# Gates and values of seven sequences by seven block products in a recurrent-attention block

## The chip, the cores and the metric

The kernel runs on one core of one Trainium2 chip. The metric is the device time of one execution in microseconds (us). A core has TensorE (PE, matrix products; its weight loads are listed apart as PEld), VectorE (DVE), ScalarE (ACT), GpSimd (POOL) and SyncE (SP, which here issues most DMAs). Each engine takes its instructions in the order in which they were traced and waits on semaphores for the others.

## The reference

Eight sequences of 1024 positions and 512 channels are normalized to `xn`. An attention without softmax over positions, with three decay rates and a gate, gives `s`; a feed-forward block whose weights are looked up in a table of 16 entries gives `g`; the result is `x + s * g`. The part that the change touches:

```python
q = x @ Wq                                  # x is the normalized input, 512 -> 128
gate = softmax(x @ Wg, axis=-1)             # 512 -> 3
for i in range(3):
    k = x @ Wk[i]; v = x @ Wv[i]            # 512 -> 128 each
    w = decay[i] ** max(t - s - 1, 0) * (later > earlier)
    scores = einsum('btd,bsd->bts', q, k) * w
    blended += gate[..., i:i+1] * einsum('bts,bsd->btd', scores, v)
s = blended @ Wo * out_scale
```

All arithmetic is in float32.

## The kernel before

Phase 1 (`phase_1`, L719) makes q^T, k^T, values and gates, runs the attention in chunks of 128 positions, from the last chunk to the first, and looks up the feed-forward weights. Phase 2 (L813) is the feed-forward block, with products of blocks nested twice, and the final sum.

Phase 1 has nine rounds, the passes of the loop over b at L759. In round b, `newer` projects sequence b, `older` runs the chunks of sequence b-1, `ending` finishes the projection of sequence b-1, `following` begins sequence b+1, and `build_some` adds steps of the table look-ups, which run on VectorE. A round has eight passes k (chunk c = 7 - k), and each pass three slots. All of these are generators, advanced by one step at fixed places of a slot, so the order of every engine's work is written out by hand and then held (`keep_order`). `defer(n, f)` issues f at the n-th later `tick`, of which there is one at each slot.

What the change and the steps of the prediction touch:

- `transpose` (L449) turns a chunk of the normalized input into `xnT` by four transposes (tile pt).
- `values` (L455): four matmuls of a chunk give 387 columns, three times 128 values and three gate logits (tile pv, L459), and ScalarE copies them into `v_sb` (L462). `newer` calls it in the third slot of every pass.
- `softmax` (L464), once for each half of 512 positions, makes the gates from the last three columns. VectorE and ScalarE do it in two steps, in the second and third slot of a half's first pass. Then `write` (L481) stores them transposed in DRAM by a DMA of single words on SP. Only for one half of sequence 0 does TensorE transpose them (`turn`, L485). A DMA on SP (L498) later spreads them over the partitions (tile ga).
- `features` (L500) makes q^T and k^T of a half by seven block products instead of eight (Strassen's scheme in Winograd's form). The matrix of weights is cut into 2 by 2 blocks, `xnT` likewise; t1 to t4 are sums of blocks of `xnT` (VectorE), s1 to s4 of weights (GpSimd). Each product is four matmuls of 256 columns (L520), into one of four PSUM banks pa, pb, pe, pc; copies on ScalarE and three-operand sums on VectorE (L552, L555) carry them on. `features(1)` runs in passes 4 to 7 of its own round, `features(0)` as `ending` in passes 0 to 3 of the next. A half's t1 is in the second slot of its first pass, product 5, which reads t1, in the third.
- `chunks` (L639), one step in each slot. First: pk, three transposes of k, copied to ks with a scale on ScalarE (L673). Second: psc = k^T q for three decays (L677), which VectorE weights into pr (L679); then `gated(c - 1)` multiplies gates and q for the next chunk (ga, L652, on VectorE; qb, L656, on GpSimd). Third: pu (L687), the update of the state; po (L701), first from the state, then from pr and the values; its copy into bl (L702) and, every four chunks, a DMA of bl on ScalarE's queue (L704).

In a slot the order is: `newer`, `following`, `older`, look-ups in the first; `ending` (two steps), `newer`, look-ups, `older`, look-ups in the second; `ending`, `newer`, `older` in the third.

Of the kernel before, what the change touches and what calls it, by code (L numbers as in the profile page):

```python
# [9 lines left out]
F32 = mybir.dt.float32  # L10
# [7 lines left out]
P = 128  # L18
# [30 lines left out]
def recurrent_block(ctx: ExitStack, tc, x, wq, wk, wv, wo, wg, decay_logits, out_scale, lut, gidx, uidx, didx, out):  # L49
# [33 lines left out]
    NQ = NO // 4  # L83
    EPS = 1e-5
# [24 lines left out]
    def more_weights(wvg_sb, wqk_sb):  # L109
        nc.scalar.dma_start(out=wvg_sb[:, :, NI * D :], in_=wg.rearrange("(c p) d -> p c d", p=P))  # L110
        for i in range(NI):
            nc.scalar.dma_start(
                out=wvg_sb[:, :, i * D : (i + 1) * D], in_=wv[i].rearrange("(c p) d -> p c d", p=P)
            )
# [46 lines left out]
    zero = const.tile([NI, P], F32)  # L161
# [7 lines left out]
    def tables(room):  # L169
# [8 lines left out]
        nc.gpsimd.memset(e_c, float(P))  # L178
        nc.gpsimd.memset(zero, 0.0)
# [222 lines left out]
    def project(b, pools, sides, kept):  # L402
# [5 lines left out]
        xp, xnp, tp, att = pools  # L408
        wvg_sb, wqk_sb, wqs = sides
        xnT = xnp.tile([P, NV, T], F32, name=f"xnT{b}", tag="xnT")  # L410
        mean, rstd, shift = (small.tile([P, NC], F32, name=f"{k}{b}", tag=k) for k in ("mean", "rstd", "shift"))
        v_sb = att.tile([P, NC, NI * D + NI], F32, name=f"v{b}", tag="v")
        gt = v_sb[:, :, NI * D :]
# [9 lines left out]
        def statistics(c):  # L423
# [10 lines left out]
            else:  # L434
                junk = small.tile([P, V], BF16, name=f"junk{b}_{c}", tag="junk", bufs=1)
# [19 lines left out]
        def values(c):  # L455

            pv = p_c.tile([P, NI * D + NI], F32, name=f"pv{b}_{c}", tag="c")
            for v in range(NV):
                nc.tensor.matmul(  # L459
                    pv, lhsT=xnT[:, v, ts(c, P)], rhs=wvg_sb[:, v, :], start=(v == 0), stop=(v == NV - 1)  # L460
                )
            nc.scalar.copy(v_sb[:, c, :], pv)  # L462

        def softmax(hf):  # L464
# [15 lines left out]

            def write():  # L481
# [3 lines left out]
            def turn():  # L485
# [3 lines left out]
                gs = small.tile([n * NI, P], F32, name=f"gs{b}_{hf}", tag="gs", bufs=1)  # L489
# [3 lines left out]
            ga = gates[-1]  # L493
            if (b, hf) == (0, 1):
# [3 lines left out]
            defer(6, lambda: nc.sync.dma_start(out=ga, in_=there.partition_broadcast(P)))  # L498

        def features(hf):  # L500
# [14 lines left out]
            pa, pb, pe, pc = (p_a.tile([P, 2, H], F32, name=f"{r}{b}_{hf}", tag=r) for r in ("pa", "pb", "pe", "pc"))  # L515
# [12 lines left out]

            there = xs_d[b][:, :, ts(hf, H)]
            nc.vector.tensor_tensor(t1, b12, b11, ALU.subtract)  # L530
            yield
            product(pa, 1, True)
            nc.scalar.copy(pb, pa)
            nc.vector.tensor_tensor(t2, b22, t1, ALU.subtract)
            nc.sync.dma_start(out=there[:, 0:4, :], in_=xnT[:, :, ts(2 * hf, H)])
            yield
            product(pe, 5, True)
            nc.scalar.copy(c21, pe)
            nc.vector.tensor_tensor(t3, b22, b12, ALU.subtract)
            nc.sync.dma_start(out=there[:, 4:8, :], in_=xnT[:, :, ts(2 * hf + 1, H)])  # L540
            yield
            product(pb, 6)
            nc.scalar.copy(pc, pb)
            nc.scalar.copy(c12, pb)
            nc.vector.tensor_tensor(t4, b21, t2, ALU.subtract)
            defer(2, lambda: nc.sync.dma_start(out=there[:, 8:16, :], in_=ts_.rearrange("p a b u -> p (a b) u")))
            yield
            product(pa, 2)
            nc.scalar.copy(c11, pa)
            yield  # L550
            product(pc, 7)
            nc.vector.tensor_tensor(c22, pc, c21, ALU.add)  # L552
            yield
            product(pe, 3)
            nc.vector.tensor_tensor(c12, pe, c12, ALU.add)  # L555
            yield
            product(pc, 4)
            nc.scalar.copy(c21, pc)
            yield
# [25 lines left out]
        yield  # L585
        before = 2 if b == 0 else 3
        lag = 1 if b == 0 else 0
        for k in range(NC):
# [8 lines left out]
            if b == 0 and k == 0:  # L597
                warm_up(5)
            yield
            if k == NC // 2:  # L600
# [943 lines left out]
```

## Time and profile before

| | us |
|---|---|
| median of the three runs (2082.22 to 2082.50) | 2082.42 |
| profiled execution | 2085.11 |
| its span, first to last instruction | 2083.3 |
| phase 1 in it, to the first product of phase 2 | 586.9 |
| rounds 1 to 7, from the first psc of sequence 0 (47.25) to that of sequence 7 (552.83) | 505.6 |
| round 8, from there to the end of phase 1 | 34.1 |

A row of a group reads: line, engine, operation, output <- inputs, shapes, count | busy us, mean ns of one | idle us of the engine just before them, and what ended it. Matmuls overlap, so the mean of one is longer than the distance between two starts. A row of the cut by time gives, for each engine, its busy us in that stretch and the number of its instructions, then TensorE's granted clock, the share of the DMA engines and GB/s. A row of the timeline gives the start, the length and the number of merged instructions. A row of the waits gives who waited for whom, us in total, times and the longest.

### The profile page before, as it was taken

What the parts mean: (1) busy time and instruction counts of PE and PEld (TensorE: products, weight loads), DVE (VectorE), ACT (ScalarE), POOL (GpSimd) and SP (SyncE); (2) the same over time, 40 slices, a digit from 0 to 9 for tenths busy, and PEclk for the clock granted to TensorE, in tenths of its full rate; (3) what the DMA queues carried; (4) which work ended last, traced back from release to release, by engine and by line L of the source; (5) the groups of instructions that cost most, each with busy time, mean ns of one, the idle gap of its engine ahead of it and who ended that gap; (6) DMA issues with size and microseconds to landing.
All of it is one profiled execution on the core that took longest, in us unless ns stands there. A gap on an engine that the chain in (4) does not pass through costs nothing.

```text
span 2083.3 us, 32914 instructions
## 1 busy us (share of the span) xinstructions
PE 2068.4 (99%) x12043; PEld 1755.3 (84%) x12043; DVE 1462.5 (70%) x2246; ACT 944.1 (45%) x2133; POOL 1043.8 (50%) x1042
## 2 busy tenths in 40 slices
PE   9999999999999999999999999999999999999999
PEld 7887888788888888897888888888978888797887
DVE  8989898788458775675577557656755765675567
ACT  4767766676444424423442442344144324423531
POOL 4554665244356446516543751755275255627442
PEclk9999999999999999999999999999999999999999
DMA  9866778756764734463464447345544734464442
GB/s 231 157 176 181 188 192 178 202 126 185 168 225 154 249 142 155 168 243 133 155 228 160 154 154 261 129 160 192 198 153 153 261 129 151 170 232 144 150 162 104
DMA packets 178494, 367.23 MB, mean 176 GB/s; under 512 B 37871, under 2 KB 113278, under 8 KB 178334
## 3 DMA queue, kind: packets, MB, share of 16 engines
q1 hardware_dynamic: 161734, 338.11, 53.0%
q10 hardware_dynamic: 12120, 12.34, 1.9%
q0 software_dynamic: 4480, 14.68, 1.7%
q8 instruction: 96, 1.57, 0.3%
q14 instruction: 64, 0.52, 0.1%
HBM read 285.36 MB, written 79.73 MB: 175 GB/s over the span
## 4 chain that ended last, share of the span: by engine, by line
PE 92%; DVE 5%; DMA 2%; issue 1%; ACT 0%; SPq 0%; POOL 0%; ACTq 0%; DVEq 0%; POOLq 0%
PE s L963 34%; PE pv L459 6%; PE sE L963 6%; PE s11d L1226 5%; PE s12d L1226 5%; PE s21d L1226 5%; PE po L701 3%; PE pd L1344 3%; PE ps L1351 3%; PE sEd L1226 2%; PE pe L520 2%; PE fs L875 2%; PE pc L520 2%; PE pa L520 2%; PE psc L677 2%; PE pu L687 1%
## 5 line engine op out<-in xcount | busy, mean ns | idle before, releaser
L963 PE MATMUL s<-xs,wq 128*128 128x256 f32 x3264 | 731.6, 379 | 0.6 <-DVE s L986 0.6
L963 PEld LDWEIGHTS s<-xs,wq 128*128 128x128 f32 x3264 | 619.3, 190 | 96.8 <-issue 7.6
L986 DVE TENSOR_TENSOR s<-s,e 128x512 f32<-128x512 f32 x136 | 95.1, 699 | 188.9 <-ACT s L985 188.9
L1315 POOL TENSOR_TENSOR cu<-cu 128x256 f32<-128x256 f32 x32 | 35.1, 1097 | 328.7 <-DVE cl L1314 328.7
L459 PE MATMUL pv<-wvg_sb,xnT 128*128 128x387 f32 x512 | 177.4, 488 | 0.0
L848 POOL TENSOR_TENSOR xs<-xs 128x256 f32<-128x256 f32 x224 | 171.1, 790 | 8.5 <-PE fr L890 4.0
L990 DVE TENSOR_TENSOR sE<-s,e 128x512 f32<-128x512 f32 x136 | 95.0, 699 | 103.2 <-PE s L963 103.1
L1058 POOL TENSOR_TENSOR u<-u,e 128x512 f32<-128x512 f32 x64 | 81.7, 1299 | 147.7 <-DVE u L1054 129.2
L981 ACT COPY e<-sE 128x512 f32<-128x512 f32 x136 | 79.6, 585 | 139.6 <-PE sE L963 137.1
L963 PE MATMUL sE<-xs,wq 128*128 128x256 f32 x544 | 139.6, 379 | 0.0
L459 PEld LDWEIGHTS pv<-wvg_sb,xnT 128*128 128x128 f32 x512 | 94.2, 190 | 53.7
L1062 POOL TENSOR_TENSOR h<-h,u 128x512 f32<-128x512 f32 x64 | 81.1, 1288 | 108.1 <-DVE u L1069 108.1
L438 POOL TENSOR_SCALAR rstd<-rstd 128x1 f32<-128x1 f32 x56 | 26.1, 467 | 209.8 <-ACT junk L437 208.8
L974 ACT COPY s<-s 128x512 f32<-128x512 f32 x136 | 77.5, 570 | 110.2 <-PE s L963 105.1
L985 ACT COPY s<-s 128x512 f32<-128x512 f32 x136 | 77.5, 570 | 97.5 <-PE s L963 97.5
L1226 PE MATMUL s12d<-wdd,z 128*128 128x128 f32 x896 | 118.4, 275 | 0.6 <-ACT s12d L1248 0.6
L963 PEld LDWEIGHTS sE<-xs,wq 128*128 128x128 f32 x544 | 103.4, 190 | 14.1
L1226 PEld LDWEIGHTS s12d<-wdd,z 128*128 128x128 f32 x896 | 109.0, 192 | 0.8 <-ACT s12d L1248 0.8
L227 DVE TENSOR_SCALAR leaf<-idx,lut_x,lut_sb 128x1024 int32<-128x1024 int32 (+2 forms) x119 | 107.7, 930 | 0.0
L656 POOL TENSOR_TENSOR qb<-ga,q_tab 128x384 f32<-128x384 f32 x56 | 75.4, 1346 | 56.1 <-DVE ga L652 26.4
L244 DVE COPY_PREDICATED leaf<-bit,leaf 128x1024 f32<-128x1024 uint8 (+2 forms) x68 | 93.5, 1375 | 1.7
L1355 POOL TENSOR_TENSOR gx<-gx,cu 128x512 f32<-128x512 f32 x32 | 40.7, 1277 | 82.0 <-DVE cu L1353 64.5
(272 smaller groups left out, 4554.4 us busy)
## 6 DMA issues: line engine op xcount, KB each, us to landing
wq<-quadd SPq DMA_DIRECT2D x112, 896.0 KB, 4.5
wdd<-wdd SPq DMA_DIRECT2D x56, 896.0 KB, 5.0
xs<-xsd SPq DMA_DIRECT2D x56, 512.0 KB, 6.4
wq<-quadd SPq DMA_DIRECT2D x48, 448.0 KB, 3.8
x<-in_x SPq DMA_DIRECT2D x64, 256.0 KB, 6.3
xsd<-xnT SPq DMA_DIRECT2D x32, 512.0 KB, 10.9
xsd<-ts SPq DMA_DIRECT2D x16, 1024.0 KB, 16.1
gx<-in_x SPq DMA_DIRECT2D x64, 256.0 KB, 6.4
```

Source lines behind the costliest of these rows:

```text
L227: nc.vector.tensor_scalar(o.bitcast(I32), iv, lut_x[:rows, k, :], lut_i[:rows, k, 0:1], ALU.bitwise_and, ALU.bitwise_xor,)
L244: nc.vector.copy_predicated(o, bits[level - 1][:rows, :n], t[:rows, :n])
L459: nc.tensor.matmul(pv, lhsT=xnT[:, v, ts(c, P)], rhs=wvg_sb[:, v, :], start=(v == 0), stop=(v == NV - 1))
L520: nc.tensor.matmul(ps[:, j, :], lhsT=lhs[k][:, v, ts(j, D)], rhs=rhs[k][:, v, :], start=start and j == 0 and v == 0, stop=False, skip_grou ...
L848: nc.gpsimd.tensor_tensor(o, x1, x2, ALU.subtract)
L963: nc.tensor.matmul(self.t[n][:, ts(a, H)], lhsT=self.w[:, a, (0, 1, 6, 3, 4, 5, 2)[i - 1], :], rhs=self.xs[:, X_OF[self.ks[a]], D_OF[i], : ...
L981: nc.scalar.copy(self.e, self.t[3])
L986: nc.vector.tensor_tensor(self.t[1], self.t[1], self.e, ALU.add)
L990: nc.vector.tensor_tensor(self.t[3], self.t[2], self.e, ALU.add)
L1058: nc.gpsimd.tensor_tensor(o[:, n], o[:, n], other[:, n], ALU.add)
L1062: nc.gpsimd.tensor_tensor(of_h(half, n), of_h(half, n), two(other[:, n]), ALU.mult)
L1226: nc.tensor.matmul(self.t[n][:, ts(a, P)], lhsT=self.lhs[i][:, e, ts(a, P)], rhs=self.w[:, e, D_OF[i], :], start=start and a == 0 and e == ...
```

## The change

For sequences 1 to 7 (`by_sevens`) the values and the gate logits are no longer made chunk by chunk. The 387 columns, logits now first, and one column of zeros make 388, two blocks of VW = 194. With the same blocks and sums of `xnT` as q^T and k^T, seven block products (four matmuls of 194 columns each) give values and logits of a half. GpSimd makes the sums of their weights once, in pass 0 of round 1.

The seven products of the values and the seven of q^T and k^T stand in one list: values 1, 5, 6, 2, 3, 7, then q/k 1, values 4, and q/k 5, 6, 2, 7, 3, 4. t1 and the first product are in the first slot of a half's first pass, then follows one product a slot, two in the third slot of the half's first and third pass. `ending` is advanced once in each slot. The values of a half go where its features go, so those of positions 0 to 511 move into the next round.

The gates' first step stands at value product 3, the second at 7; at value product 4 TensorE turns them, ScalarE copies them into a buffer of ks and stores them, and the spread follows at the next tick. To make room the discarded output of the statistics becomes U8, a bl tile holds two chunks and is stored every two, and a tile of zeros moves into another's room. The core of the diff (the parts that only reorder columns and rename arguments are cut):

```diff
+    VW = (NI * D + NI + 1) // 2
...
-        v_sb = att.tile([P, NC, NI * D + NI], F32, name=f"v{b}", tag="v")
-        gt = v_sb[:, :, NI * D :]
+        by_sevens = b > 0
+        v_sb = att.tile([P, NC, 2 * VW], F32, name=f"v{b}", tag="v")
+        gt = v_sb[:, :, :NI]
...
-                junk = small.tile([P, V], BF16, name=f"junk{b}_{c}", tag="junk", bufs=1)
+                junk = small.tile([P, V], U8, name=f"junk{b}_{c}", tag="junk", bufs=1)
...
-                gs = small.tile([n * NI, P], F32, name=f"gs{b}_{hf}", tag="gs", bufs=1)
+                gs = chk.tile([n * NI, P], F32, name=f"gs{b}_{hf}", tag="ks")
                 nc.scalar.copy(gs, pg)
                 nc.scalar.dma_start(out=there, in_=gs)
-            if (b, hf) == (0, 1):
+            if by_sevens:
+                yield
+                turn()
+                defer(1, spread)
+                yield
+                return
+            if hf:
                 defer(3, turn)
             else:
                 defer(2, write)
-            defer(6, lambda: nc.sync.dma_start(out=ga, in_=there.partition_broadcast(P)))
+            defer(6, spread)
...
+            def product_of_v(ps, k, start=False):
+                for m in range(2):
+                    for v in range(2):
+                        nc.tensor.matmul(
+                            ps[:, m, :],
+                            lhsT=rhs[k][:, v, ts(m, P)],
+                            rhs=w_of_v[k][:, v, :],
...
+            def step(k, multiply, width, to):
+                pa, pb, pe, pc = (lambda r=r: bank(r, width) for r in ("pa", "pb", "pe", "pc"))
+                o11, o12, o21, o22 = to
+                if k == 1:
+                    multiply(pa(), 1, True)
+                    nc.scalar.copy(pb(), pa())
+                elif k == 5:
+                    multiply(pe(), 5, True)
+                    nc.scalar.copy(o21, pe())
+                elif k == 6:
+                    multiply(pb(), 6)
+                    nc.scalar.copy(pc(), pb())
+                    nc.scalar.copy(o12, pb())
+                elif k == 2:
+                    multiply(pa(), 2)
+                    nc.scalar.copy(o11, pa())
+                elif k == 7:
+                    multiply(pc(), 7)
+                    nc.vector.tensor_tensor(o22, pc(), o21, ALU.add)
+                elif k == 3:
+                    multiply(pe(), 3)
+                    nc.vector.tensor_tensor(o12, pe(), o12, ALU.add)
+                else:
+                    multiply(pc(), 4)
+                    nc.scalar.copy(o21, pc())
...
+            steps = [(k,) + of_qk for k in (1, 5, 6, 2, 7, 3, 4)]
+            if by_sevens:
...
+                first = [(k, product_of_v, VW, to) for k in (1, 5, 6, 2, 3, 7, 4)]
+                steps = first[:6] + steps[:1] + first[6:] + steps[1:]
+                half = softmax(hf)
+                after = {4: half, 5: half, 7: half}
             nc.vector.tensor_tensor(t1, b12, b11, ALU.subtract)
             yield
+            for n_step, one in enumerate(steps):
+                step(*one)
+                if sums:
+                    sums.pop(0)()
+                next(after.get(n_step, iter(())), None)
+                yield
...
+            if by_sevens and k >= NC // 2:
+                if k == NC // 2:
+                    of_half = features(1)
+                    next(of_half)
+                next(of_half)
             yield
+            if k >= NC // 2 and by_sevens:
+                some_of(of_half, 1)
+                yield
+                some_of(of_half, 2 - k % 2)
+                yield
+                continue
...
         of_half = features(0)
         for k in range(NC // 2):
+            if by_sevens:
+                some_of(of_half, 2 if k == 0 else 1)
+                yield
+                some_of(of_half, 1)
+                yield
+                some_of(of_half, 2 - k % 2)
+                yield
+                continue
...
-        n_of = NC // NHALF
+        n_of = 2
...
                     next(newer, None)
+                    if k < NC // 2:
+                        next(ending, None)
...
                     if k < NC // 2:
-                        for _ in range(2):
-                            next(ending, None)
+                        next(ending, None)
...
+                    if (b, k) == (1, 0):
+                        nc.gpsimd.memset(wvg_sb[:, :, NI * D + NI :], 0.0)
+                        sums_of_weights(wvg_sb, wvs, VW)
```

## Prediction before the run

> **What bounds the kernel now.** I read the busy shares first, then the busy times cut at the rounds of phase 1 (round b is pass b of the loop of phase_1: sequence b is projected, the chunks of b-1 run beside it), then the instructions of TensorE in order, then the waits. Busy shares:
>
> ```profile
> PE 2068.4 (99%) x12043; PEld 1755.3 (84%) x12043; DVE 1462.5 (70%) x2246; ACT 944.1 (45%) x2133; POOL 1043.8 (50%) x1042
> ```
>
> TensorE looks like the only bound. The cut by rounds, limits at the first transpose of each, says otherwise for phase 1 (to 586.9 us):
>
> ```profile
> core 0: us, PE busy (x) PEld busy (x) DVE busy (x) ACT busy (x) POOL busy (x), PEclk, DMA share, GB/s
> 44.80:117.70 72.90, 71.40 (x411) 59.47 (x410) 68.58 (x81) 50.78 (x135) 41.94 (x40) 1.00 0.83 167
> 117.70:190.90 73.20, 71.95 (x412) 59.36 (x411) 66.86 (x83) 49.80 (x132) 43.12 (x38) 1.00 0.64 186
> 190.90:263.80 72.90, 71.48 (x412) 59.33 (x411) 67.36 (x83) 49.97 (x132) 38.12 (x35) 1.00 0.69 186
> 263.80:335.30 71.50, 71.36 (x411) 59.38 (x410) 68.21 (x83) 49.87 (x132) 40.72 (x37) 1.00 0.80 177
> 335.30:408.20 72.90, 71.44 (x411) 59.15 (x411) 54.35 (x83) 49.85 (x132) 30.95 (x34) 1.00 0.90 209
> 408.20:479.10 70.90, 70.90 (x411) 59.27 (x410) 57.46 (x78) 49.78 (x132) 34.98 (x35) 1.00 0.62 157
> 479.10:550.00 70.90, 70.90 (x411) 59.27 (x411) 50.91 (x69) 44.83 (x118) 34.14 (x29) 1.00 0.60 145
> ```
>
> See the first and the fourth number of a row. A round without a stall takes 70.9 us, all of it TensorE's. But in rounds 1 to 4 VectorE is busy for 67 to 69 us as well: the table look-ups of the FFN weights, at fixed places of the order, fill it. In rounds 5 to 7 it has 13 to 20 us left.
>
> Two pages bear on that first row. The Trainium skill, "Perfetto Trace Analysis", section Identifying the Most-Contended Engine, holds matmul busy time for a poor measure of how near TensorE is to its limit, and occupancy for a fair one on VectorE. By the 99% alone the change would be worth what it takes off TensorE, 16 us; by the rounds it is not, and the rounds decide.
>
> TensorE in round 6, in order:
>
> ```profile
> 429.06 0.83 PE L677 MATMUL psc<-ga,qk 128*128 128x128 f32 x6
> 429.72 1.89 PE L520 MATMUL pe<-xnT,wqs 128*128 128x256 f32 x8
> 431.45 2.77 PE L459 MATMUL pv<-wvg_sb,xnT 128*128 128x387 f32 x8
> 434.06 0.83 PE L687 MATMUL pu<-v,ks 128*128 128x128 f32 x6
> 434.73 0.83 PE L701 MATMUL po<-qb,R 128*128 128x128 f32 x6
> 435.40 0.83 PE L701 MATMUL po<-pr,v 128*128 128x128 f32 x6
> 436.07 0.60 PE L452 MATMUL pt<-ident,x 128*128 128x128 f32 x4
> 436.50 0.49 PE L670 MATMUL pk<-ident,qk 128*128 128x128 f32 x3
> ```
>
> Start to start gives prices: a product of q^T, k^T 1.73 us, the values of a chunk 2.61, psc, pu and each half of po 0.67, pt 0.44, pk 0.33. Per instruction (a float32 matmul is two): 326 ns for 387 columns, 216 for 256, 112 for 128. The view also shows a **cover**: the second half of po needs pr, which VectorE makes from psc. From the end of psc to there TensorE has 5.5 us of other work, half of it the values. VectorE is behind by 2 to 4 us in rounds 1 to 4 (pr begins 3.0 us after psc ends in round 3, chunk 6; 4.3 in round 2, chunk 2), and the cover hides it.
>
> **The change, part by part.** *Values on TensorE.* Before, 64 instructions of 326 ns a sequence: 20.9 us. After, 14 products of 8 instructions with 194 columns. 194 lies between 128 and 256, so between 112 and 216 ns; on the line between the rows it is 165 ns: 1.32 us a product, 18.5 a sequence. Saved: 2.4 us in each of seven sequences, 17 in all. Fourteen turns of one instruction (the one pg of the trace is a single 128-column transpose, so about 0.11 us) cost 1.5.
>
> "Perfetto Trace Analysis", section Matmuls, calls larger matmuls more efficient than smaller ones, which speaks against products half as wide. The rows show 0.84 ns a column at 387, 0.84 at 256 and 0.88 at 128; with the price of 128 a sequence would save 1.8 us and not 2.4.
>
> *Where it goes.* Values of chunks 0 to 3 move from their own round into the next (features(0) runs as `ending`). A full round then needs 70.9 - 2.4 + 0.2 = 68.7 us of TensorE. Round 1 loses a whole sequence of values and gets back half: 59.3. Round 8, which has only chunks of sequence 7 and the end of its features, gains seven products: **+9.3 us**. That round is dense now (from 553 to 587 us I find 1.5 us of stalls), and all of phase 2 stands behind it in TensorE's order, so the 9.3 are paid in full.
>
> *VectorE.* Each half adds two sums of 388 columns from PSUM. Rows:
>
> ```profile
> L679 DVE TENSOR_TENSOR pr<-psc,w_tab 128x384 f32<-128x384 f32 x56 | 30.8, 550 | 20.5 <-PE psc L677 20.5
> L552 DVE TENSOR_TENSOR qk<-pc,qk 128x512 f32<-128x512 f32 x14 | 9.7, 691 | 29.2 <-ACT shift L446 25.2 <-PE pc L520 4.0
> ```
>
> 0.55 us each, 2.2 a round (1.1 in round 1). Nothing is taken from VectorE. Busy time rises to 69.7, 69.1, 69.6 and 70.4 us in rounds 1 to 4, over the 68.7 (59.3) of TensorE: there VectorE is the bound, so a gain can only come out of its idle time. Its idle stretches over 0.3 us there sum to 16.8 us, and nearly all stand where the look-ups pause (5.7 at 150 us, 4.9 at 213): it has nothing else to do then, and they stay.
>
> *The cover shrinks.* The values no longer stand between psc and po. With one product of 1.73 us it is 3.1 us (chunks 6, 4, 2; 2.4 at chunk 0), with two 3.3 to 4.8.
>
> *A ledger* adds this up. From psc of one chunk to the next, TensorE takes P plus a stall of max(0, lag + 0.6 - cover), 0.6 being pr; lag, the time from psc's end to pr's start, becomes lag + W - P - stall, not below 0. W is VectorE's time from pr to pr in the trace, less its idle stretches over 0.3 us, plus what the change adds. Where a half starts, product 5 waits for t1, so lag over 1.5 (before: 2.0; 4.6 at k = 4, where values stood ahead) is a stall too; these are chosen by eye from rounds 2 and 3.
>
> ```
> k   P before/after   cover before/after   W added
> 0    8.83   8.02        4.7   3.3          +0.80
> 1    9.51   8.32        5.5   3.1          -0.69
> 2    9.50  10.36        5.5   4.8          +0.69
> 3    7.78   7.79        3.8   3.1          +0.30
> 4    9.51   8.68        5.5   3.9          +0.80
> 5    9.50   8.32        5.5   3.1          -0.69
> 6    9.18  10.03        5.5   4.8          +0.69
> 7    7.11   7.13        3.2   2.4          +0.30
> ```
>
> Signs differ since qk's sums, t3, t4 and the softmax move by a slot. Round 3 after, W from the trace 10.55, 1.62, 12.62, 8.05: lag 1.5; k=0 no stall, lag 1.5 + 11.35 - 8.02 = 4.8; k=1 stall 2.4, then VectorE, with 0.9 us to do, waits 5; k=2 lag 3.0; k=3 stall 0.5, and 1.5 more for t1; k=5 stall 1.7. All eight: 74.8 us (before, by the same ledger 71.8; the trace has 72.9). Rounds 1 to 7 before: 73.6, 72.3, 71.8, 70.9 and three of 70.9, sum 501.4; the trace has 505.6, so the ledger is short by 4. After: 72.7, 74.7, 74.8, 71.9, 68.7, 70.3, 69.4, sum 502.3. **Rounds 2 and 3 lose what 5 to 7 win: +0.9 us.**
>
> *Costed at nothing, with both ends.* ScalarE: four more evictions of 0.49 us a round, two more bl stores, two copies of gs; it is busy for 50 of 71 us, but a turn's store sat on its queue in round 0:
>
> ```profile
> 30.26 0.25 ACT L490 COPY gs<-pg 12x128 f32<-12x128 f32 x1
> 32.07 0.57 ACTq L491 DMA_DIRECT2D gTd<-gs  x1
> 32.68 0.48 ACT L462 COPY v<-pv 128x387 f32<-128x387 f32 x1 [2.17 <-DMA xsd<-xnT]
> ```
>
> 2.2 us in which the copies behind it (ks for pu) wait. At k = 2 and 6 ks would end about 8.7 us after the transposes begin and TensorE has 8.1 us until pu: 0 to 0.7 us each, 13 times, 0 to +9. SP: fourteen writes of 1536 single words go (6 KB, median 14.6 us to land; SP waited 106 us for them). The spread stays at the same place of SP's order with the x loads behind it, but its source is now made one slot earlier instead of five. VectorE's wait for it:
>
> ```profile
> DVE ga L652 <- DMA ga<-gTd: 13.8, 4, 5.8
> ```
>
> That can vanish or grow: -4 to +4, and 0 is taken. POOL's four weight sums and the memset (about 5 us in round 1, rows of 256 columns at 1.1 us) lie in its 31 idle us, four slots ahead of their use. The U8 junk, zero's room and the new column order I put at nothing, between -1 and +1.
>
> Sum: +0.9 + 9.3 + 0.1 (turn in round 8) = +10.3. The profiled run took 2085.1 us, its span 2083.3; span after 2093.6. On the median of the runs, 2082.4, that is **2092.7**.
>
> **Rivals.**
> - *Transfer to round 8 and VectorE as the bound* (forecast), 2087 to 2099: chance 0.50.
> - *VectorE absorbs its sums in its idle stretches*: rounds 1 to 4 stay at the 290.5 us of the trace, 5 to 7 win 7, round 8 pays 9.4: 2085. For it: only 7 idle stretches carry the 16.8 us, and TensorE could arrive earlier at them. 0.18, and 0.16 of it within 0.2% (4.2 us, about what can be told from no change).
> - *TensorE stays the bound* (faster): lag never outgrows the new cover; every round falls to 68.7 and stalls go, -16 us, 2066; in part, 2074. It decides if rounds 2 to 4 end under 70 us. Against it: 69 to 70 us of VectorE in each. 0.12.
> - *In-order chains*: each slot now holds one product whose sum or copy stands behind look-ups or the gs store; one more us in half the slots of rounds 1 to 7, +9 to +15: 2098 to 2108. 0.20.
> - *The products are no cheaper* (216 ns an instruction, as with 256 columns): 24.2 us a sequence for 18.5, and 5.7 more in seven: 2110 and over. Under 0.02, counted with the last.
>
> The range leaves out the faster case and the far end of the last: 2079 to 2106. Faster 0.12, within 0.2% 0.16, slower 0.72.
>
> **What would show it.** Right: 194-column instructions 165 ns apart; rounds 2 and 3 at 73 to 76 us with TensorE idle before po's second half (pr) and product 5 (t1); VectorE 95% busy there; rounds 5 to 7 near 69.5; round 8 at 43 instead of 34 us. Wrong: rounds 2 to 4 under 70, or round 8 unchanged.

## The result, and the profile after

The kernel after takes **2117.1 us** (median of 5 runs, 2115.2 to 2118.6), the one before 2082.5 beside it: ratio 1.0166, 95% interval 1.0151 to 1.0181. It is slower, as forecast, but by 34.6 us and not by 10.3.

The profiled execution's span is 2115.1 us (before 2083.3). The two profiles thus differ by 31.8 us and not by 34.6, because the profiled execution of before took 2.6 us more than its median; what follows explains the 31.8. Cut from the first psc of a sequence's chunks to that of the next (round 8: to the first product of phase 2):

| us | round 1 | 2 | 3 | 4 | 5 | 6 | 7 | 8 | phase 2 |
|---|---|---|---|---|---|---|---|---|---|
| before | 73.6 | 72.5 | 72.9 | 71.6 | 72.9 | 70.9 | 71.2 | 34.0 | 1496.4 |
| forecast after | 72.7 | 74.7 | 74.8 | 71.9 | 68.7 | 70.3 | 69.4 | 43.4 | as before |
| after | 75.4 | 77.7 | 83.1 | 73.7 | 71.1 | 74.8 | 73.1 | 42.7 | 1496.4 |

Phase 2 and round 8 are as forecast. The miss is all in rounds 1 to 7: 23.3 us more than before, where the ledger had 0.9. Busy shares of the whole, as the page of the kernel after has them:

```profile
PE 2068.6 (98%) x12393; PEld 1810.0 (86%) x12393; DVE 1474.1 (70%) x2274; ACT 960.6 (45%) x2175; POOL 1052.1 (50%) x1047
```

TensorE's busy time is the same as before to 0.2 us, although the change takes 16 us of work off it. So part of its instructions must have become longer. (The account below finds 10.0 us of that. The other 6 are an effect of counting: an instruction counts as busy to its end, also where no other follows at once, so that of 37.6 us of new stalls only 31.6 show as idle time.) The cut by rounds (limits at the first transpose of a round; rounds 2, 3, 5 and 6 of the kernel after) says why:

```profile
118.60:196.20 77.60, 72.70 (x461) 68.58 (x459) 67.02 (x87) 52.30 (x138) 38.99 (x37) 0.96 0.51 167
196.20:279.40 83.20, 72.36 (x462) 68.12 (x462) 68.75 (x86) 52.28 (x138) 40.78 (x35) 0.96 0.49 162
...
353.60:424.90 71.30, 69.69 (x463) 65.88 (x462) 52.65 (x84) 52.16 (x138) 32.51 (x34) 1.00 0.56 190
424.90:499.40 74.50, 71.32 (x475) 67.48 (x473) 60.33 (x85) 53.54 (x142) 36.30 (x35) 1.00 0.50 157
```

Look at the clock, the third number from the end: 0.96 in rounds 2 and 3, where all rows of before had 1.00. And VectorE (the third busy time) is not full in rounds 2 and 3: 67.0 of 77.6 and 68.8 of 83.2 us. Nor is it in rounds 5 and 6; yet round 5 is only 1.6 us shorter than before (71.3 for 72.9), and round 6 is 3.6 us longer (74.5 for 70.9).

An **account** of rounds 1 to 8 separates the causes. Each distance from one TensorE instruction to the next is compared with the dense price of its columns (128: 110 ns, 194: 165, 256: 216, 387: 327). An excess of 0.8 to 1.25 times the price is put down to half clock, any other to stalls; that is good to about half a microsecond.

| us, rounds 1 to 8 | instructions at dense price | stalls | half clock | sum |
|---|---|---|---|---|
| before | 525.6 | 13.2 | 0.9 | 539.7 |
| after | 509.9 | 50.8 | 10.9 | 571.6 |
| difference | -15.7 | +37.6 | +10.0 | +31.9 |
| forecast (15.5 off TensorE; the rest of +10.3 as stalls) | -15.5 | +25.8 | 0 | +10.3 |

So the saving is there to 0.2 us. What failed is 12 us of stalls too few, and 10 us of half clock that the prediction does not mention. TensorE's waits in the kernel after (us in total, times, the longest):

```profile
PE pe L549 <- DVE ts L612: 16.7, 9, 7.2
PE po L787 <- DVE pr L765: 13.0, 11, 2.8
PE pu L773 <- ACT ks L759: 3.6, 4, 2.0
PE pb L549 <- ACT pb L563: 2.2, 4, 1.2
PE psc L763 <- ACT v L566: 1.9, 1, 1.9
```

Before, the first two were 2.7 and 2.4. These are product 5 waiting for t1, and po's second half for pr, the two waits that the forecast named. The last three are for ScalarE, 7.7 us.

The longest stall, 7.4 us in round 3, shows a chain that the sum put at nothing. First product 5, then VectorE ahead of it (the number in brackets is the idle time before the instruction, and what ended it):

```profile
243.64 2.96 PE L549 MATMUL pe<-wvs,ts 128*128 128x194 f32 x8 [7.22 <-DVE ts L612]
```

```profile
239.00 0.56 DVE L738 TENSOR_TENSOR ga<-ga,qk 128x384 f32<-128x384 f32 x1 [5.65 <-DMA ga<-gTd]
...
242.91 0.68 DVE L612 TENSOR_TENSOR ts<-xnT 128x512 f32<-128x512 f32 x1
```

TensorE waits for t1, which stands in VectorE's queue behind three look-up steps and a product with the gates; that product waited 5.65 us for the spread to land. SyncE's issues, after and then before, tell why it was late:

```profile
225.78 0.53 SPq L313 DMA_DIRECT2D quadd<-wgu  x1
...
230.21 0.61 SPq L486 DMA_DIRECT2D ga<-gTd  x1
```

```profile
216.34 0.34 SPq L498 DMA_DIRECT2D ga<-gTd  x1
...
219.37 0.53 SPq L312 DMA_DIRECT2D quadd<-wgu  x1
```

Before, the spread (ga<-gTd) left ahead of the store of looked-up weights. Now its source is made later, and it stands behind two such stores (the one shown and one at 229.60), which waited 9.6 and 3.2 us for GpSimd to finish those weights: issued at 230.2, landed at 239.0.

Then the clock. The stretch around the end of this stall, and the next one:

```profile
242.00:248.00 6.00, 4.36 (x16) 4.36 (x17) 4.87 (x7) 0.48 (x1) 1.39 (x1) 0.50 0.00 0
249.00:255.00 6.00, 6.00 (x46) 5.98 (x45) 5.03 (x6) 3.45 (x10) 1.44 (x1) 1.00 0.11 16
```

At a granted clock of 0.50, 16 instructions take 4.36 us; at 1.00, 46 take 6.00. (Their widths are mixed; products of 194 columns stand 325 ns apart in the first row and 165 in the second.) There are five such stretches in the rounds of the kernel after, each 3.4 or 6.8 us long (from 60.5, 77.6, 159.5, 241.4 and 504.3 us), and none before. The Trainium skill, "TensorE: Matmul & The Clock Gate", section Part 1: The HAM clock gate, gives the gate as half clock after an idle window of about 3.4 us. The stretches are one or two times that long, but here the window need not be idle, and the length of the stall alone does not decide: in after, stalls of 3.0 us (to 60.7) and 2.1 us (to 76.7 and to 502.9) were followed by half clock, stalls of 2.3 us (to 214.3) and 2.1 us (to 465.2) were not.

The kept traces show what does decide. In each trace the stretches begin whole multiples of 3.413 us apart (in after 16, 21, 45, 69 and 146 of them after the clock's first rise). Cut a trace into slots at these points, and count in each slot how long TensorE works, every instruction at its dense price:

| slot, us from the start | the stall in it | TensorE at work | half clock from the slot's end |
|---|---|---|---|
| after, 57.1 to 60.5 | 3.0 us, to 60.7 | 16% | yes |
| e11 (below), 56.0 to 59.4, and the next | 3.0 us, to 61.0, parted between the two | 41% and 50% | no |
| after, 500.9 to 504.3 | 2.1 us, to 502.9 | 36.5% | yes |
| after, 210.7 to 214.1 | 2.3 us, to 214.3 | 37.3% | no |

In the 16 traces of this case there are some 9600 slots that began at full clock. All 42 with TensorE at work for under 37.3% were followed by half clock. Of all others one was, at 37.4%, and three between 37.3 and 37.6% were not. So the same stall costs its clock or not by where it falls on the slots.

### The profile page after: what moved, and what is told of

Same layout as the page of the kernel before. It is cut to its first block, busy times and chain, and to the rows that moved or that the text cites. A ratio compares the mean times of both kernels' runs of the same rounds, so it can differ in the third digit from the quotient of the medians.

```text
span 2115.1 us, 33775 instructions
## 1 busy us (share of the span) xinstructions
PE 2068.6 (98%) x12393; PEld 1810.0 (86%) x12393; DVE 1474.1 (70%) x2274; ACT 960.6 (45%) x2175; POOL 1052.1 (50%) x1047
## 4 chain that ended last, share of the span: by engine, by line
PE 81%; DVE 3%; ACT 1%; issue 1%; ACTq 0%; DVEq 0%
PE s L1054 33%; PE sE L1054 6%; PE s11d L1317 5%; PE s12d L1317 5%; PE s21d L1317 5%; PE pd L1435 3%; PE ps L1442 3%; PE sEd L1317 2%; PE fs L966 2%; PE po L787 2%; PE fr L981 1%; PE pe L537 1%; PE s11d L1328 1%; PE s12d L1328 1%; PE s21d L1328 1%; PE sEd L1328 1%
## 5 line engine op out<-in xcount | busy, mean ns | idle before, releaser
L1153 POOL TENSOR_TENSOR h<-h,e 128x512 f32<-128x512 f32 x64 | 81.2, 1301 | 0.0
L1149 POOL TENSOR_TENSOR e<-e,u 128x512 f32<-128x512 f32 x64 | 79.8, 1283 | 0.0
```

What stands on the lines that cost most here:

```text
L1149: nc.gpsimd.tensor_tensor(o[:, n], o[:, n], other[:, n], ALU.add)
L1153: nc.gpsimd.tensor_tensor(of_h(half, n), of_h(half, n), two(other[:, n]), ALU.mult)
```

## The experiments

Theory after seeing this: look-ups at fixed places make VectorE late, the new order has fewer microseconds of cover, and each long stall costs its clock as well. Rivals: ScalarE's queue; the late spread; the side edits (turn of the gates, wider store). All kernels are timed against before on the same chip. The rounds' sums and accounts:

| us | median | ratio (95% interval) | rounds 1-4 | 5-7 | 8 | stalls | half clock |
|---|---|---|---|---|---|---|---|
| before | 2082.5 | | 290.6 | 215.0 | 34.0 | 13.2 | 0.9 |
| after | 2117.1 | 1.0166 (1.0151-1.0181) | 309.9 | 219.0 | 42.7 | 50.8 | 10.9 |
| e1 after, no look-ups | 2091.8 | 1.0042 (1.0026-1.0059) | 284.6 | 212.4 | 42.7 | 26.1 | 3.8 |
| e2 before, no look-ups | 2082.4 | 0.9996 (0.9986-1.0005) | 283.7 | 212.3 | 34.1 | 4.2 | 0.3 |
| e3 spread first | 2117.5 | 1.0167 | 310.8 | 220.6 | 42.7 | | |
| e4 other slots | 2145.3 | 1.0304 (1.0289-1.0320) | 325.6 | 229.0 | 44.1 | 73.1 | 15.7 |
| e5 e1 + copies first | 2084.7 | 1.0006 (0.9997-1.0016) | 283.4 | 208.8 | 42.8 | 19.8 | 5.2 |
| e6 after, look-ups moved | 2104.2 | 1.0099 (1.0084-1.0114) | 291.0 | 224.2 | 44.4 | 44.9 | 4.9 |
| e7 before, look-ups moved | 2088.8 | 1.0026 (1.0016-1.0035) | 283.8 | 215.1 | 44.1 | 14.5 | 2.9 |
| e8 before + side edits | 2110.3 | 1.0129 (1.0114-1.0144) | 313.2 | 216.8 | 34.4 | 30.9 | 6.3 |
| e9 e8, turn elsewhere | 2101.1 | 1.0089 (1.0075-1.0103) | 303.1 | 216.4 | 34.4 | 23.2 | 3.7 |
| e10 before, better moved | 2080.1 | 0.9987 (0.9978-0.9996) | 284.8 | 216.3 | 34.1 | 9.4 | 0.4 |
| e11 after, turn earlier | 2106.4 | 1.0113 (1.0099-1.0126) | 300.7 | 215.8 | 42.7 | 45.5 | 3.9 |
| e12 after, both orders | 2112.7 | 1.0141 (1.0128-1.0155) | 294.7 | 229.9 | 42.7 | 46.2 | 11.4 |
| e13 e8, third place | 2108.2 | 1.0121 (1.0104-1.0138) | 313.0 | 217.1 | 34.4 | 30.8 | 6.6 |
| e14 e11 + look-ups moved | 2103.5 | 1.0100 (1.0085-1.0115) | 290.3 | 225.1 | 42.7 | 45.0 | 3.2 |

**e1, e2: without the look-ups.** Of each look-up only its first leaf is left; masks, other leaves and selections go, so the feed-forward weights are not those of the tables.

```diff
-                leaf(o, k)
+                if not light or k == 0:
+                    leaf(o, k)
...
-            nc.vector.copy_predicated(o, bits[level - 1][:rows, :n], t[:rows, :n])
+            if not light:
+                nc.vector.copy_predicated(o, bits[level - 1][:rows, :n], t[:rows, :n])
```

> The changed kernel with nearly all table look-ups of phase 1 left out (of the some 20 VectorE steps of a look-up only the first leaf and its mask stay, so the FFN weights are wrong); every other instruction stays. Theory (VectorE is what TensorE waits for: it is full in rounds 1 to 4, and pr and t1 come late): the stalls of 41 us and the half-clock stretches go, phase 1 is bound by TensorE, and the kernel takes 2058 to 2066 us, 14 to 17 us less than the unchanged kernel with the same look-ups left out. Rival (ScalarE's evictions and the gate chain hold TensorE up by themselves): 2075 us or more, and stalls before pu and product 6 stay.

> The kernel before with the same look-ups left out; the partner of the run above. Theory: it loses only its own 8 us of stalls, 2073 to 2080 us. Rival (something else than VectorE): 2080 to 2083 us.

Of after's 25 us that went, the rounds lost 32 (round 1 begins 6.7 us later in e1, and 7.1 in e2, whose rounds become fully dense at 70.9; so e2's total stays where it was, above the 2073 to 2080 of its expectation). The later start is in round 0: in e2 the store of the gates leaves ScalarE's queue only at 37.7 us, 7.3 behind the copy that makes its source; TensorE waits 4.2 us for a copy of xnT behind it, and 6.8 us at half clock come with that. VectorE's load is the larger cause: rounds 1 to 8 of after are 32 us longer than those of before, but those of e1 only 9.6 longer than those of e2, so the look-ups make 22 of the 32. It is not the only one. e1 came out at 2092, far above the 2058 to 2066 expected, with 26 us of stalls, and its rounds 1 to 7 take 497.0 us, e2's 496.0, although TensorE has 24 us less to do in them. In round 3 of e1 the late spread is still there (TensorE waits 2.8 us). And here is a stall that comes back in rounds 2 and 4 to 7, ScalarE first, then TensorE (in e1 lines are three further down):

```profile
372.44 0.30 ACT L451 ACTIVATE shift<-mean,rstd 128x1 f32<-128x1 f32 x1
372.77 0.81 ACT L452 ACTIVATE x<-x,shift,rstd 128x512 f32<-128x512 f32 x1
373.49 0.61 ACT L441 ACTIVATE junk<-x 128x512 uint8<-128x512 f32 x1
...
374.95 0.47 ACT L566 COPY pb<-pa 128x388 f32<-128x388 f32 x1
```

```profile
375.48 1.25 PE L552 MATMUL pb<-wvs,ts 128*128 128x194 f32 x6 [1.68 <-ACT pb L566]
```

Product 6 adds to the copy of product 1. That copy could run from 371.5 on, when product 1 is done, but is traced behind the next chunk's normalization and statistics, which ScalarE does first.

**e3: the spread ahead in the list of deferred issues.**

```diff
-                defer(1, spread)
+                later.insert(0, [1, spread])
```

> The changed kernel with one edit: the DMA that spreads the gates goes ahead of the other DMAs of its tick on SP, where in the change it stands behind stores that wait for GpSimd (SP issued it at 230.2 us in round 3 instead of about 222, VectorE waited 5.7 us for it and TensorE 7.4 us for t1). Theory that the queue position is one cause among several: 8 to 12 us less, 2105 to 2109 us, round 3 near 75 us. If VectorE would be late anyhow: 2114 to 2118 us. If it is the main cause: under 2100 us.

Nothing changed: the spread still left at 231.2, since the stores ahead of it belong to earlier ticks. The run says nothing of what the wait is worth.

**e4: other counts of products in the slots**, (1,0,3), (0,1,2), (1,1,2), (0,1,2) in a half's four passes, so that t1 has more time.

> The changed kernel with the same fourteen products in other slots: first, second and third slot of the four passes hold 1,0,3 / 0,1,2 / 1,1,2 / 0,1,2 products (in the change 1,1,2 / 1,1,1 / 1,1,2 / 1,1,1). This lengthens the work between psc and the second half of po to 4.4 to 4.8 us and puts product 5 two slots behind t1. Theory (short cover): waits for t1 fall from 16.7 us to under 4, waits for pr from 13 to about 7, half-clock stretches from 24 us to under 10: 2092 to 2102 us. Rival (VectorE is simply too full, wherever the products stand): 2112 us or more, the waits only change their places.

The two waits shrank as expected (product 5's for t1 from 16.7 us to nothing, po's for pr from 13.0 to 4.7), and the kernel became 28 us slower. That is what its rival says, 2112 us or more with the waits only in other places. Product 4 of the values now follows product 7 by one slot, and so waits for VectorE's sum, which stands behind look-ups:

```profile
PE pc L549 <- DVE v L576: 28.7, 10, 4.8
```

The wait on VectorE moves to the next edge that has no cover.

**e5: e1, with the products' copies ahead on ScalarE's queue.** In a pass's first slot the products come before normalization and statistics, and `ending` before `newer`.

```diff
             transpose(c)
+            if by_sevens and k >= NC // 2:
+                if k == NC // 2:
+                    of_half = features(1)
+                    next(of_half)
+                next(of_half)
             if c > 0:
                 normalize(c - 1)
...
-                    next(newer, None)
                     if k < NC // 2:
                         next(ending, None)
+                    next(newer, None)
```

> The changed kernel without the look-ups (as the first experiment), and in the first slot each product step stands ahead of the normalization and the statistics instead of behind them, so that its copy into the next bank is ahead of 2.8 us of work on ScalarE's queue. Theory (ScalarE's order is the second cause: product 6 waits 1.8 us once a round for the copy pb<-pa): these stalls and part of the waits for ks go, rounds 2 to 7 at 68.7 to 69.5 us, 2076 to 2081 us. Rival (the wait only moves on to ks and pu, or the products' own chain is too long): 2086 to 2092 us.

The wait for pb goes (8.9 us to nothing), ks takes some of it (pu's wait 3.1 to 7.0). 7 us faster than e1, short of the 11 to 16 expected. Not all of it is ScalarE: in round 3 the spread now leaves at 215.9, one store ahead of where it was, and the round falls by 4.1 us. Rounds 2 and 5 to 7, in which nothing else was seen to move, fall by 0.7 to 1.7 us each. Rounds 1 and 4 rise by 1.7 and 2.0; in round 4 the exponential of the gates waits 2.3 us for VectorE and now has ks behind it. ScalarE's order is a cause of its own, but a small one; and without any look-up, in the better order, the change still only draws level with before.

**e6, e7: look-ups moved** out of rounds 1 to 4 (46 steps for 52), 56 in rounds 5 to 7, the rest in round 8, in after and in before.

```diff
+                    elif b < 5:
+                        steps = ((1, 1, 4), (1, 1, 4), (1, 1, 4), (1, 1, 3))[k % 4]
                     elif b < B:
-                        steps = ((1, 1, 4), (1, 2, 4), (1, 2, 4), (1, 2, 3))[k % 4]
+                        steps = (1, 2, 4)
                     else:
-                        steps = (1, 0, 0)
+                        steps = (1, 1, 0)
```

> The changed kernel with the look-ups spread evenly: 46 steps in each of rounds 1 to 4 instead of 52, 56 in rounds 5 to 7, the rest in round 8. Nothing is left out. Theory (VectorE full in rounds 1 to 4): rounds 1 to 4 fall by 8 to 15 us together, rounds 5 to 7 rise by up to 4: 2102 to 2110 us. Rival (the share of VectorE doesn't matter, only single late instructions do): 2113 us or more.

> The kernel before with the look-ups spread in the same way; partner of the run above. Its stalls in rounds 1 to 4 sum to about 7 us. Theory: 2077 to 2082 us. Rival: the look-ups moved into rounds 5 to 8 cost there what they save: 2082 to 2086 us.

e6's total lies where it was expected, but both parts are larger than expected: six steps fewer take 19 us off rounds 1 to 4 of after (7 off those of before), and four more add 5 to rounds 5 to 7. Of the 19, 10.4 are in round 3, where the edit does a second thing: the store of looked-up weights comes later (238.2), so that the spread, issued at 213.9, is ahead of it again. In the other three rounds after gains 8.5 us and before 4.9; after is the more sensitive to VectorE's load. e7 missed: its rounds 1 to 4 became dense, but round 8 took 10 us more. There psc waited 6.7 us for the gated product of a late spread, and 6.8 us at half clock came with it.

**e8, e9, e13: the side edits alone.** Before, with the turn by TensorE for sequences 1 to 7, bl stored every two chunks, and the narrower scratch. The three differ in when the turn is issued (e8 `defer(3)`; e9 1 and 2; e13 2 and 3 ticks, second half and first).

```diff
-        n_of = NC // NHALF
+        n_of = 2
...
-            if (b, hf) == (0, 1):
+            if b > 0 or hf:
                 defer(3, turn)
```

> The kernel before with all of the change but the block products: gates turned by TensorE in sequences 1 to 7 (store on ScalarE's queue, spread where it was), bl stored every two chunks, the discarded output in U8. Theory (these are harmless): 2080 to 2084 us. Rival (each turn's store holds ScalarE's queue by up to 2.2 us): 2087 us or more.

> The kernel before with the change's side edits and no block products of the values: the gates of sequences 1 to 7 turned by TensorE and stored from ScalarE, the wider store of the outputs, the narrower scratch type. Unlike in the run before it of this kind the turn stands at the head of a slot, where its PSUM buffer comes from a po that is long done. Theory that the loss of the change lies in where the block products stand: the side edits cost nothing by themselves, 2080 to 2086 us, all rounds 70.9 to 73.7 as before, round 8 at 34. Rival that turning and storing the gates on ScalarE's queue costs time: 2090 us and above, spread over rounds 2 to 8.

> Once more the kernel before with the side edits alone (gates of sequences 1 to 7 turned by TensorE and stored from ScalarE, wider store of the outputs, narrower scratch type), now with the turn two slots behind the softmax of the gates, and never ahead of the values' product. In the two runs before, the turn itself or the product behind it waited for VectorE (pg for the gates 16.4 us, the values' product for pr 18.0 us). Theory that it was the place alone: both waits under 3 us, 2080 to 2087 us. Rival that the turn costs wherever it stands (its copy and store on ScalarE's queue, its buffer of the three): 2092 us and above.

All three are slower by 18 to 28 us, so the theory that these edits are free by themselves fell three times. In e8 the values' product waits for pr (18.0 us): pg takes one of three PSUM buffers, and the values' product, next in the ring, then gets the one that pr still reads. In e9 pg itself waits for the gates (16.4). In e13 both do:

```profile
PE pv L459 <- DVE pr L681: 10.5, 7, 2.6
PE pg L488 <- DVE g L477: 8.2, 5, 3.6
```

In the old order, TensorE never waited for the softmax: SyncE did. A turn gives it an edge to VectorE, 2 to 4 us at a time. In the change as made the turn has two slots of distance, and no wait of pg is in TensorE's list. So these runs do not price the side edits within the change; they show the same mechanism a third time. The wider store and the narrower scratch were not run apart; no wait of these runs names either.

**e10: the look-ups moved better, in before**: 46 steps in rounds 1 to 4, 60 in 5 to 7, round 8 as it was.

```diff
+                    elif b < 5:
+                        steps = ((1, 1, 4), (1, 1, 4), (1, 1, 4), (1, 1, 3))[k % 4]
                     elif b < B:
-                        steps = ((1, 1, 4), (1, 2, 4), (1, 2, 4), (1, 2, 3))[k % 4]
+                        steps = ((2, 2, 4), (1, 2, 4))[k % 2]
```

> The kernel before with 46 look-up steps in each of rounds 1 to 4, 60 in each of rounds 5 to 7 (52 in each before), and none added to round 8. Theory that VectorE is late in rounds 1 to 4 alone, where the dispatch and the wide adds stand beside the look-ups: rounds 1 to 4 dense at 283.8 us together as in the run with 46 steps (290.6 before), rounds 5 to 7 at 71.6 or less each, round 8 at 34.0, sum 47.4 + 283.8 + 214.5 + 34.0 + 1496.4, thus 2074 to 2078 us, faster than both kernels. Rival that 60 steps are too many for rounds 5 to 7 too (74 us each, the 4 us that a stall and its clock cost): 2081 to 2086.

2080.1 us, 0.13% under before, interval 0.04% to 0.22%: **faster than both kernels**, if by little. Rounds 1 to 4 give 5.8 us; rounds 6 and 7 take 1.5 and 1.8 back, with four waits of po of 0.6 to 1.0 us each. The theory's 2074 to 2078 missed by 2 us: rounds 5 to 7 took 1.8 us more than it allowed, since 60 steps are a little too many there, and rounds 1 to 4 1.0 more.

**e11: the turn, and with it the spread, one slot earlier** in after.

```diff
-                after = {4: half, 5: half, 7: half}
+                after = {4: half, 5: half, 6: half}
```

> The kernel after with the turn of the gates, and with it the spread, one slot earlier. Theory that the late spread of round 3 (issued at 230.2 behind stores that waited for POOL) makes its 7.4 us stall and 6.9 us at half clock: round 3 falls from 83.0 to 73 to 76, the other rounds stay within 2, total 2105 to 2111 us. Rival that one slot is too little to bring the spread past the stores: round 3 stays at 82 to 84, total 2114 to 2119 us.

Hit: 10.7 us off, of which 7.9 in round 3 (83.1 to 75.1). SyncE in that round:

```profile
214.85 0.34 SPq L486 DMA_DIRECT2D ga<-gTd  x1
...
224.85 0.52 SPq L313 DMA_DIRECT2D quadd<-wgu  x1
```

The spread is 15 us earlier, again ahead of the stores. In round 3 the account loses 6.0 us of stalls and 1.9 of half clock. In round 1 it is the other way: half clock falls by 2.7 us and stalls grow by 2.7, so nothing is won there. Over all, stalls fall by 5.3 and half clock by 7.0. So 5.1 us of half clock went in rounds at which the edit was not aimed. The stalls of 3.0 and 2.1 us in round 1 are still there (to 61.0 and 76.9); they fall otherwise on the slots, and pass at full clock. That part of the gain is luck. Round 6 falls by 2.2 us, just over the 2 foreseen.

**e12: after with e5's order and e10's look-ups.**

> The kernel after with two edits: ScalarE's queue takes the copies of the products ahead of the next chunk's normalization and statistics, and VectorE has 46 look-up steps in rounds 1 to 4, 60 in rounds 5 to 7, none in round 8. Theory that the loss of the rounds is these two and the clock they cost: against the run with fewer steps alone (2104.2) the waits for the copy pb go (7.0 us) and round 8 falls back from 44.4 to 42.7, so 2090 to 2097 us; what is left above 2082.5 is then round 8's 8.7 us and little else. Rival that 60 steps in rounds 5 to 7 make VectorE late there (77 us and more each, as 56 steps made of round 7): 2100 to 2108 us.

Both missed: 2112.7. pb's waits went, but pu now waits 21.1 us for ks, with this on ScalarE's queue:

```profile
275.99 0.21 ACT L474 ACTIVATE g<-g 128x12 f32<-128x12 f32 x1 [2.76 <-DVE g L473]
...
279.08 0.86 ACT L759 ACTIVATE ks<-pk,k_tab 128x128 f32<-128x128 f32 x3
```

The exponential of the gates waits 2.8 us for VectorE, and now stands ahead of the normalization, the statistics and ks instead of behind the statistics. With look-ups, an order that is better without them (e5) passes VectorE's lag on through ScalarE; e5 itself has one such stall, in round 4. The order with the look-ups where the change has them was not run.

**e14: e11 and e10's look-ups in after.**

> The kernel after with the two edits that each took about 11 us off it: the turn of the gates one slot earlier, and 46 look-up steps in rounds 1 to 4, 60 in rounds 5 to 7, none in round 8. Alone they took 12.4 and 13.7 us off rounds 1 to 7, of which some 8 are the same (round 3). Theory that both act on separate waits but for that: 2115 - 18 = 2097, thus 2093 to 2101 us. Rival that 60 steps are too many for rounds 5 to 7 of this kernel, wherever the copies stand on ScalarE's queue (74.7 to 78.8 us each in the run with the copies ahead): 2103 to 2110 us.

2103.5, no better than e6's 2104.2. Rounds 1 to 7 lose 13.5 us, where the two edits alone lose 12.4 (e11) and 13.7 (e6). So they are not two causes that add up: with fewer look-ups in e6 the spread is no longer late in round 3 (72.7 us), so that little is left there for the earlier turn to mend, and that turn brings a wait of its own (pg for the gates, 8.0 us in 7).

## Why the prediction was wrong in size

The direction was right, and so were round 8 and the kind of waits. The time came out 24.4 us above the forecast and 11 above the range (to 2106). By the steps:

- **Price of the products**: right. 194 columns are 165 ns apart, and TensorE's own work fell by 15.7 us (15.5 forecast).
- **Round 8**: right, +8.6 us (9.4 forecast), and phase 2 stands behind it unchanged.
- **Waits for t1 and pr**: the right ones. The ledger let stalls grow by 25.8 us in all; they grew by 37.6. By rounds, with half clock left out, the growth of rounds 1, 2 and 5 is within half a microsecond of the ledger's; the surplus is in round 3 (4.8 us), round 6 (4.4), 7 (1.7) and 4 (1.2). The ledger used mean work per slot, and a lag chosen by eye for t1, and so does not see what stands just ahead of t1 or pr in one place. (Its seven rounds after, as printed, add up to 502.5 and not 502.3, which changes nothing.)
- **"There VectorE is the bound"**: not as meant. The sign for it, VectorE 95% busy in rounds 2 and 3, did not come: 86 and 83% (96 in rounds 1 and 4). VectorE is late at single places and idle at others; it is not full.
- **"Rounds 5 to 7 near 69.5"**: wrong, 73.0 on average, with VectorE busy for only 53 to 60 us of them. The prediction took spare time on an engine for absence of waits. e1 takes 6.6 us off these three rounds (look-ups), e5 another 3.6 (ScalarE's order).
- **"Costed at nothing", ScalarE, 0 to +9**: measured as 7.7 us of TensorE's waits (ks, pb, v). The place was wrong too: the prediction names the gs store ahead of ks. That store takes 0.3 us on the queue and leaves ScalarE idle for 0.4 behind it (13 times); the copy of product 1 that stands behind the statistics costs 2.2 us here, and 8.9 in e1.
- **"Costed at nothing", the spread, -4 to +4**: one stall of 7.4 us where 1.5 was counted, and the clock behind it; with the spread earlier (e11) round 3 is 7.9 us shorter. "The same place of SP's order" was true, and its source one slot earlier instead of five was seen, but not what then stands ahead of it on that queue.
- **The clock**: not a term of the sum at all, and 10.0 us. This is the step that failed: the sum prices a stall at its own length, and leaves out that TensorE may run at half clock behind it. Of the 24.4 us of the miss 11.8 are stalls and 10.0 the clock; the rest is almost all the difference of profile and median named above. For costs such as the two above, 7.7 and 5.9 us, the range had room at its upper end (13.3 us over the forecast); for the clock it had none. It is not the clock alone, though: without its 10.0 us the time would be 2107, still a microsecond above the range. How much clock a given sum of stalls costs is in part chance (10.9 us on 50.8 of stalls in after, 3.9 on 45.5 in e11).

The rival named "in-order chains" (2098 to 2108) was the nearest: e1, e4 and e12 show such chains. It too lacks the clock. The offer of the change was 15.7 us of TensorE's time (24 less in rounds 1 to 7, 8.5 more in round 8). Stalls on VectorE and ScalarE and their clock took more than that back.

Left open: a version of the change below 2082 us. The best with all look-ups is e14 at 2103.5. Its rounds 1 to 7 have 43 us of stalls, of which 32 are five kinds of waits of 3 to 8 us each. What the turn, the wider store and the narrower scratch cost within the change is open too.

## What to carry to other kernels

In a stream that is already dense, cutting an engine's work can be worth nothing where that work was the cover of a wait, as in rounds 1 to 7 here: list for each operand that comes from another engine how much independent work stands between its maker and its reader, and what stands ahead of the maker in its queue, before and after. Price a stall of more than some 2 us with the half clock that may follow it (here 10 us of clock on 38 of new stalls), and before crediting an edit with a gain, take the clock's part out: it can come and go with the place of a stall. And an order that is better without one engine's load need not be better with it (e5, e12): try edits in the presence of all the others.

## What the runs showed of the hardware

- Half clock began at the end of a slot of 3.413 us in which TensorE had worked for less than about 37%, and nowhere else while a kernel ran (43 cases in 16 traces, all in phase 1); the slots run on evenly through each trace. It follows, as an estimate, that a single stall under 2.1 us (63% of a slot) passes at full clock and one over 4.3 us (twice that) never does; between them its place decides (one of 3.7 us passed in e13, one of 2.1 us did not in after). At half clock products of 194 columns took 325 ns each instead of 165.
- Products of 194 columns cost the same per column (0.85 ns) as those of 256 and 387: halving their width lost nothing on TensorE.
- The spread of 12 rows over 128 partitions took 8.8 us from issue to landing in round 3 of after, at a DMA share of 0.94 in that stretch. In before the 16 spreads took 5.5 to 8.7 us: this one was late mainly because it was issued late.
